# Mixture-of-experts layers of a macaron block: two second-choice scatters under way among the experts, and three experts in place of two that complete the output's rows

## The chip, the cores and the metric

The kernel runs on one core of one Trainium2 chip. A core has a matrix engine (TensorE, here PE, whose weight loads the profile lists as PEld), a vector engine (VectorE, DVE), a scalar engine (ScalarE, ACT), GpSimd (POOL) and SyncE (SP), and 16 DMA engines that they share. Each of the five executes its own queue of instructions in order and waits on semaphores. In this kernel SP issues the plain transfers and POOL the indirect ones (rows scattered or gathered by an index for each partition).

The metric is the device time of one execution, in microseconds (us): the median of several runs. A profiled execution gives the trace; its own time stands beside it.

## The reference

A macaron block: a feed-forward layer with weight 0.5, a gated delta-rule attention, and the same feed-forward layer again. The two feed-forward layers are mixtures of 8 experts; each token goes to its two best experts, and every choice has a capacity of 640 tokens for each expert. The part that the change touches is this, with N = 4096 tokens, D = 128 and a hidden width of 512:

```python
capacity = max(int(N / E * CAPACITY_FACTOR), 1)              # 640
top_k_probs, top_k_idx = jax.lax.top_k(router_probs, TOP_K)  # 2 choices
out = jnp.zeros_like(x_flat)
for k in range(TOP_K):
    eid, ew = top_k_idx[:, k], top_k_probs[:, k]
    ...
    pos = jnp.take_along_axis(pos_all, eid[:, None], axis=1)[:, 0]
    valid = pos < capacity
    disp = jnp.zeros((E, capacity, D)).at[eid, pos_c].add(jnp.where(valid[:, None], x_flat, 0.0))
    gate = jax.nn.silu(jnp.einsum('ecd,efd->ecf', disp, wi_gate))
    up = jnp.einsum('ecd,efd->ecf', disp, wi_up)
    expert_out = jnp.einsum('ecf,edf->ecd', gate * up, wo)
    tok_out = expert_out[eid, pos_c]
    out = out + jnp.where(valid[:, None], ew[:, None] * tok_out, 0.0)
...
x = x + 0.5 * _L0_ffn_ref(_layernorm(x), ...)
x = x + _L0_attn_ref(_layernorm(x), ...)
x = x + 0.5 * _L0_ffn_ref(_layernorm(x), ...)
```

## The kernel before

**Layout.** The tokens lie in SBUF as `x`, four groups `g` of 128 partitions x 8 tokens x 128 numbers. Each feed-forward layer ("layer 1" and "layer 2" below) has four tables in HBM: `disp` for each choice `k` (8 experts x 640 slots, a row of 128 numbers, the token's number and its two weights) and `back` for each choice (one row of results for each token).

**Dispatch.** `Routing.dispatch` (L520) sends one tile of 128 tokens to its slots with an indirect scatter on POOL. The slots of different scatters never overlap. To let them run side by side, the table is given as 32 views that count as disjoint (L373); a scatter writes view `(g * NC + n) % abreast`, and two scatters to one view are kept in order by a wait of the second for the landing of the first. With `abreast` at its full value no scatter waits for another; with 1 each waits for the one before it. The first choices are sent in full before the experts begin. The second choices are sent by `second` (L569), with `abreast` 1: in layer 1 eight tiles before expert 0 and then four with each of experts 0 to 5 (`LATER`, L861), in layer 2 four before expert 0 and then three with each of experts 0 to 3 (L1569 to L1578).

**Experts.** `experts` (L554) runs i = 0 to 15: the 8 experts on first choices, then the 8 on second choices. For each, `fetch` (L574) loads the weights `we` (768 KB, three buffers) and the 640 rows `xd` (three buffers), and `expert` (L601) transposes the rows (`ptx`, then `xdT` by ACT and DVE), computes 4 column blocks for each half of the tokens (`pg`, `pu`, `sg`, `hT`), multiplies back (`py`) in two parts of three and two tiles, weights them on DVE (`ye`, L652), and scatters the five tiles on POOL to `back` (L661). The second choices' scatters stand in POOL's queue among these: one after the first three result scatters, the others after the last two. POOL's indirect transfers are held in program order (`in_order`, L516). Expert 8's rows need all second choices landed.

**Combining.** `combine_first` (L548) loads a group of `back` for first choices and adds half of it to `x` on DVE, one group with each of experts i = 10 to 13; the addition stands behind the weighting of the expert before (`weighted`). The second choices' results of layer 1 are added in the attention stage.

**The end.** In layer 2 the last two experts (i = 14, 15) do not write to `back`. Before expert 14, `x` is stored to `kept` in HBM (L1575), and `fetch` gathers for each slot the row of `kept` of its token (`xb`, L586 to L598; both experts' rows and weights are fetched before expert 14 is computed). Within expert 14, after its last `hT`, `finish` (L1587) loads the four groups of `back` of second choices, which hold experts 8 to 13 by then, adds them to `x` and stores the whole output. The last two experts then write `0.5 * weight * py + xb` (L647) over their tokens' rows in the output (L661, to the views `self.final[1]`), so these scatters wait for the output's stores.

**Order on SP.** Loads made by `load` (L230) keep their program order on SP; the plain `xd` loads (L583) and `y` loads (L537) are placed by the scheduler.

Of the kernel before, what the change touches and what calls it, by code (L numbers as in the profile page):

```python
# [26 lines left out]
NW = 14  # L27
VPAD = 31
OUT_OF_RANGE = 1000000

# [125 lines left out]
def macaron_kernel(ctx: ExitStack, tc: tile.TileContext, x_in, consts, wts, w1b, wexp, out):  # L158
# [209 lines left out]
    class Routing:  # L368
# [178 lines left out]

        def combine_first(self, i, ex):  # L548

            g = i - NE - 2  # L550
            if 0 <= g < NG:
                self.add(g, self.results(g, 0, ex.tile([P, NC * D], F32, tag="y", name=f"y{self.layer}_{g}")))

        def experts(self, between):  # L554

            layer = self.layer
            with tc.tile_pool(name=f"ex{layer}", bufs=2) as ex:
                fetched = {}  # L560
                for i in range(2 * NE):
                    among = between(i, ex)

                    for n in (i, i + 1) if self.final and i == 2 * NE - 2 else (i,):
                        if n not in fetched:
                            fetched[n] = self.fetch(ex, *divmod(n, NE))
                    self.expert(ex, *divmod(i, NE), among, *fetched.pop(i))

        def second(self, tiles):  # L569

            for g, n in tiles:
                self.dispatch(g, 1, [n], 1)

        def fetch(self, ex, k, e):  # L574

            nm = f"{self.layer}_{k}_{e}"
            we = ex.tile([P, 3 * FF], F32, tag="we", bufs=3, name=f"we_{nm}")
            load(we, wexp[e])
            xd = ex.tile([P, JS, RW], F32, tag="xd", bufs=3, name=f"xd_{nm}")
            src = disp[self.layer - 1][k][e * ESLOT : (e + 1) * ESLOT, :]  # L580
            src = src.rearrange("(p j) d -> p j d", j=JS)
            if not (self.final and k == 1 and e >= NE - 2):
                nc.sync.dma_start(out=xd, in_=src)  # L583
                return we, xd, None
            load(xd, src)
            xb = ex.tile([P, JS, D], F32, tag="xb", name=f"xb_{nm}")  # L586
            nc.gpsimd.memset(xb, 0.0)
            for j in range(JS):
                self.in_order(nc.gpsimd.indirect_dma_start(
                    out=xb[:, j, :],  # L590
                    out_offset=None,
                    in_=self.final[0],
                    in_offset=bass.IndirectOffsetOnAxis(
                        ap=xd[:, j, D : D + 1].bitcast(I32), axis=0
                    ),
                    bounds_check=NT - 1,
                    oob_is_err=False,
                ))  # L598
            return we, xd, xb

        def expert(self, ex, k, e, among, we, xd, xb):  # L601
            nm = f"{self.layer}_{k}_{e}"
            wo = we[:, 2 * FF :].rearrange("p (f d) -> p f d", d=D)
            xdT = ex.tile([P, ESLOT], F32, tag="xdT", name=f"xdT_{nm}")
            for q, js in enumerate((range(0, 3), range(3, JS))):
                pt = psB(f"ptx_{nm}_{q}")
                w = len(js) * P
                for i, j in enumerate(js):
                    nc.tensor.transpose(pt[:, i * P : (i + 1) * P], xd[:, j, :D], ident)  # L609
                to = xdT[:, js[0] * P : js[0] * P + w]  # L610
                if q % 2 == 0:
                    nc.scalar.copy(to, pt[:, :w])  # L612
                else:
                    nc.vector.tensor_copy(to, pt[:, :w])
            if xb is not None:
                half = ex.tile([P, JS], F32, tag="half", name=f"half_{nm}")
                nc.vector.tensor_scalar(half, xd[:, :, D + 1 + k], 0.5, None, ALU.mult)
            hT = ex.tile([P, 4, ESLOT], F32, tag="hT", name=f"hT_{nm}")

            def up(f, s0, w):  # L620
                pg = psA(f"pg_{nm}_{s0}_{f}")
                nc.tensor.matmul(  # L622
                    pg[:, :w], lhsT=we[:, f * P : (f + 1) * P], rhs=xdT[:, s0 : s0 + w],
                    start=True, stop=True,
                )
                pu = psA(f"pu_{nm}_{s0}_{f}")
                nc.tensor.matmul(  # L627
                    pu[:, :w], lhsT=we[:, FF + f * P : FF + (f + 1) * P],
                    rhs=xdT[:, s0 : s0 + w], start=True, stop=True,
                )  # L630
                sg = ex.tile([P, w], F32, tag="sg", bufs=3, name=f"sg_{nm}_{s0}_{f}")
                nc.scalar.activation(sg, pg[:, :w], AF.Silu)  # L632
                made = nc.vector.tensor_tensor(hT[:, f, s0 : s0 + w], pu[:, :w], sg, ALU.mult)  # L633
                self.made = getattr(made, "ins", made)

            def down(js, among):
                py = psB(f"py_{nm}_{js[0]}")
                ye = ex.tile([P, len(js), D], F32, tag=f"ye{len(js)}", bufs=3, name=f"ye_{nm}_{js[0]}")
                for i, j in enumerate(js):
                    for f in range(4):  # L640
                        nc.tensor.matmul(  # L641
                            py[:, i * P : (i + 1) * P], lhsT=hT[:, f, j * P : (j + 1) * P],
                            rhs=wo[:, f, :], start=(f == 0), stop=(f == 3),
                        )
                if xb is not None:
                    for i, j in enumerate(js):
                        weighted = nc.vector.scalar_tensor_tensor(  # L647
                            ye[:, i, :], py[:, i * P : (i + 1) * P], half[:, j : j + 1], xb[:, j, :],
                            ALU.mult, ALU.add,
                        )  # L650
                else:
                    weighted = nc.vector.tensor_tensor(  # L652
                        ye, py[:, : len(js) * P].rearrange("p (j d) -> p j d", d=D),
                        xd[:, js[0] : js[0] + len(js), D + 1 + k].unsqueeze(2).to_broadcast(
                            [P, len(js), D]
                        ),
                        ALU.mult,
                    )
                self.weighted = getattr(weighted, "ins", weighted)
                for i, j in enumerate(js):  # L660
                    self.in_order(nc.gpsimd.indirect_dma_start(  # L661
                        out=self.final[1][(e - NE + 2) * JS + j] if xb is not None else self.rows_[k][e * JS + j],
                        out_offset=bass.IndirectOffsetOnAxis(
                            ap=xd[:, j, D : D + 1].bitcast(I32), axis=0
                        ),
                        in_=ye[:, i, :],
                        in_offset=None,
                        bounds_check=NT - 1,
                        oob_is_err=False,
                    ))  # L670
                self.second(among)

            if k == 0 or e < NE - 1:
                for s0 in (0, ESLOT // 2):
                    for f in range(4):
                        up(f, s0, ESLOT // 2)
                if xb is not None:
                    self.final[2](ex)
                down(range(0, 3), among[:1])
                down(range(3, JS), among[1:])  # L680
            else:

                for f in range(4):
                    up(f, 0, 3 * P)
                for f in range(2):
                    up(f, 3 * P, 2 * P)
                down(range(0, 2), ())
                for f in range(2, 4):
                    up(f, 3 * P, 2 * P)
                down(range(2, 3), ())  # L690
                down(range(3, JS), ())
# [172 lines left out]
    def between_1(i, ex):  # L864

        if i == 0:
            r1.second(later[: LATER[0]])

        if i in (NE + 1, NE + 2):
            clear_slots(1, i - NE - 1)  # L870
        if i in (NE + 3, NE + 4):
            clear_back(1, i - NE - 3)
        r1.combine_first(i, ex)
        return later[sum(LATER[: i + 1]) : sum(LATER[: i + 2])]
# [695 lines left out]

    def between_2(i, ex):
        if i == 0:
            r2_.second(rest[:4])
        r2_.combine_first(i, ex)
        if i == 2 * NE - 2:  # L1575
            for g in range(NG):
                load(by_group(kept[:, :])[g], x[:, g].rearrange("p n d -> p (n d)"))
        return rest[4 + 3 * i : 7 + 3 * i]  # L1578
# [13 lines left out]
            r2_.add(g, ys[g], r2_.made)  # L1592
            load(out[g], x[:, g])

    r2_.final = kept[:, :], dram_disjoint_views(out.rearrange("g p n d -> (g p n) d"), 2 * JS), finish
    r2_.experts(between_2)


# [85 lines left out]
```

## Time and profile before

| | us |
|---|---|
| median of 5 runs | 1014.78 |
| lowest, highest | 1001.78, 1020.41 |
| profiled execution | 1008.41 |
| its span | 1006.6 |
| PE busy in the span | 848.0 (84%) |
| DVE busy | 515.1 (51%) |
| ACT busy | 362.9 (36%) |
| POOL busy | 303.0 (30%) |

In the profiled execution layer 1's routing takes the first 70 us, its experts run from 74 to about 320 us, the attention to about 740 us, and layer 2's experts from 756 to 999 us. The costliest groups of POOL are the scatters of rows (L524, 128 of 991 ns) and of results (L661, 150 of 972 ns to `back`, 10 more to the output).

The profile can be read as a page (busy time of each engine, the chain of waits that ended last, groups of instructions), as busy time in chosen stretches, as a list of who waited for whom, and as instructions in order of time. In the last, a line has the start, the length, the engine, the source line, the operation, what it writes and reads, how many were merged, and in brackets the idle time of the engine before it and what ended that. "issue" is time in which the engine waited for nothing that the profile shows. PE's matmuls are pipelined and their ends are modelled. A DMA's line is the time of its issue, not of its transfer.

### The profile page before, as it was taken

The numbers are of one execution on the slowest core, as the hardware profiler recorded it, in microseconds if no ns is written. First come the engines' busy times: TensorE is split into PE (matmuls) and PEld (weight loads), VectorE is DVE, ScalarE is ACT, GpSimd is POOL, SyncE is SP. The second block draws the span as 40 slices with busy tenths as digits, with TensorE's granted clock in tenths as the row PEclk, the third lists the DMA queues.
The fourth block names the chain that finished last, engine by engine and source line by source line (L and its number), as shares of the span: only waits on it lengthen the run. The fifth ranks groups of instructions, "written<-read, shape, count | busy, mean of one in ns | idle before, by whom it ended". The sixth has DMA issues, their size and how long they took to land.

```text
span 1006.6 us, 19407 instructions
## 1 busy us (share of the span) xinstructions
PE 848.0 (84%) x7674; PEld 585.1 (58%) x7674; DVE 515.1 (51%) x1218; ACT 362.9 (36%) x710; POOL 303.0 (30%) x321
## 2 busy tenths in 40 slices
PE   3459989899995899899989989899319999999975
PEld 1247776677774344563565455455206777777754
DVE  5533333234432349579848967966623334344442
ACT  5422222122222534726724662255612223222211
POOL 2664553533225000000023003200343553332363
PEclk9999999989999799999999989999758999999998
DMA  9832425396211140320140002300042333344451
GB/s 311 306 107 75 120 85 149 127 378 217 88 54 42 33 104 1 95 47 1 49 110 26 11 13 60 80 2 2 22 126 79 106 101 114 100 147 157 147 180 46
DMA packets 36778, 101.11 MB, mean 100 GB/s; under 512 B 9296, under 2 KB 11831, under 8 KB 36688
## 3 DMA queue, kind: packets, MB, share of 16 engines
q1 hardware_dynamic: 27152, 82.47, 26.4%
q0 software_dynamic: 9536, 17.41, 5.4%
q8 instruction: 60, 0.98, 0.4%
q14 instruction: 30, 0.25, 0.1%
HBM read 48.31 MB, written 42.39 MB: 90 GB/s over the span
## 4 chain that ended last, share of the span: by engine, by line
PE 50%; issue 16%; DVE 13%; POOL 7%; ACT 6%; DMA 4%; SPq 2%; another core or an unknown queue 1%; POOLq 0%; DVEq 0%; ACTq 0%
PE pg L622 9%; PE pu L627 9%; PE py L641 8%; PE pms L1332 4%; POOL disp L524 3%; POOL back L661 3%; PE pjq L977 2%; DVE inv L1109 1%; DVE add L1104 1%; DMA disp<-row,send 1%; PE pjk L977 1%; SPq L1219 1%; PE pc L1243 1%; PE pyo L1513 1%
## 5 line engine op out<-in xcount | busy, mean ns | idle before, releaser
L524 POOL DMA_INDIRECT disp<-row,send x128 | 126.9, 991 | 477.7 <-ACT tz L1126 177.8
L633 DVE TENSOR_TENSOR hT<-pu,sg 128x320 f32<-128x320 f32 (+2 forms) x256 | 125.5, 492 | 182.1 <-PE pu L627 123.4
L661 POOL DMA_INDIRECT back<-ye,xd x150 | 145.7, 972 | 195.6 <-DVE ye L652 157.2
L622 PE MATMUL pg<-xdT,we 128*128 128x320 f32 (+2 forms) x512 | 188.0, 450 | 15.0 <-ACT xdT L612 13.8
L627 PE MATMUL pu<-xdT,we 128*128 128x320 f32 (+2 forms) x512 | 183.8, 441 | 0.8 <-issue 0.8
L632 ACT ACTIVATE sg<-pg 128x320 f32<-128x320 f32 (+2 forms) x256 | 111.6, 437 | 193.9 <-PE pg L622 117.1
L641 PEld LDWEIGHTS py<-we,hT 128*128 128x128 f32 x1280 | 148.7, 192 | 10.7 <-issue 4.4
L641 PE MATMUL py<-we,hT 128*128 128x128 f32 x1280 | 149.6, 275 | 5.3 <-issue 4.1
L622 PEld LDWEIGHTS pg<-xdT,we 128*128 128x128 f32 x512 | 96.9, 195 | 60.7 <-ACT xdT L612 21.5
L627 PEld LDWEIGHTS pu<-xdT,we 128*128 128x128 f32 x512 | 99.5, 195 | 43.8 <-issue 5.0
L1332 PE MATMUL pms<-vlag,lagw 128*32 128x512 f32 x832 | 108.3, 595 | 0.5 <-issue 0.5
L652 DVE TENSOR_TENSOR ye<-py,xd 128x256 f32<-128x256 f32 (+2 forms) x61 | 29.5, 486 | 101.2 <-PE py L641 82.1
L612 ACT COPY xdT<-ptx 128x384 f32<-128x384 f32 x32 | 15.3, 479 | 174.7 <-PE ptx L609 166.8
L1332 PEld LDWEIGHTS pms<-vlag,lagw 128*32 128x32 f32 x832 | 27.9, 108 | 40.5 <-issue 36.4
L609 PE MATMUL ptx<-cst,xd 128*128 128x128 f32 x160 | 24.5, 287 | 24.4 <-DMA xd<-disp 24.4
L1109 DVE TENSOR_TENSOR inv<-inv,add 128x31 f32<-128x31 f32 (+15 forms) x124 | 42.5, 343 | 3.8
L1104 DVE TENSOR_TENSOR add<-sys,inv 128x31 f32<-128x31 f32 (+15 forms) x124 | 42.2, 340 | 3.8
L1258 DVE TENSOR_TENSOR ui<-pc,cst 128x512 f32<-128x512 f32 x32 | 22.1, 689 | 25.6 <-PE pc L1250 19.8
L609 PEld LDWEIGHTS ptx<-cst,xd 128*128 128x128 f32 x160 | 19.6, 148 | 24.9 <-issue 24.9
L1302 ACT COPY delta<-po 128x128 f32<-128x128 f32 x32 | 8.5, 266 | 69.2 <-PE po L1295 65.7
L977 PE MATMUL pjk<-hT,wc 128*128 128x512 f32 x64 | 29.5, 603 | 0.6 <-DVE bt L361 0.6
L341 PE MATMUL pt_r<-cst,row 128*128 128x128 f32 x64 | 16.5, 388 | 14.7 <-ACT row L330 13.7
(225 smaller groups left out, 1038.2 us busy)
## 6 DMA issues: line engine op xcount, KB each, us to landing
we<-in_wexp_dram SPq DMA_DIRECT2D x32, 768.0 KB
disp<-empty SPq DMA_DIRECT2D x4, 2620.0 KB
xd<-disp SPq DMA_DIRECT2D x32, 327.5 KB
back<-zero SPq DMA_DIRECT2D x4, 2048.0 KB
y<-back SPq DMA_DIRECT2D x16, 512.0 KB
back<-ye,xd POOLq DMA_INDIRECT x150
vlag<-vbl SPq DMA_DIRECT2D x16, 143.5 KB
vlag<-vbl SPq DMA_DIRECT2D x16, 143.4 KB
```

Of the source, the lines that this page charges most:

```text
L524: sent = nc.gpsimd.indirect_dma_start(out=self.slots[k][(g * NC + n) % abreast], out_offset=bass.IndirectOffsetOnAxis(ap=send[:, k, :], ax ...
L609: nc.tensor.transpose(pt[:, i * P : (i + 1) * P], xd[:, j, :D], ident)
L622: nc.tensor.matmul(pg[:, :w], lhsT=we[:, f * P : (f + 1) * P], rhs=xdT[:, s0 : s0 + w], start=True, stop=True,)
L627: nc.tensor.matmul(pu[:, :w], lhsT=we[:, FF + f * P : FF + (f + 1) * P], rhs=xdT[:, s0 : s0 + w], start=True, stop=True,)
L632: nc.scalar.activation(sg, pg[:, :w], AF.Silu)
L633: made = nc.vector.tensor_tensor(hT[:, f, s0 : s0 + w], pu[:, :w], sg, ALU.mult)
L641: nc.tensor.matmul(py[:, i * P : (i + 1) * P], lhsT=hT[:, f, j * P : (j + 1) * P], rhs=wo[:, f, :], start=(f == 0), stop=(f == 3),)
L661: self.in_order(nc.gpsimd.indirect_dma_start(out=self.final[1][(e - NE + 2) * JS + j] if xb is not None else self.rows_[k][e * JS + j], ou ...
L977: nc.tensor.matmul(pj_.tile, lhsT=wc[:, i, k, :], rhs=hT[:, :, l0 : l0 + P], start=(k == 0), stop=(k == KQ - 1),)
L1104: nc.vector.tensor_tensor(add, sys_[:, j, k:].unsqueeze(2).to_broadcast([P, r, k]), iv[:, j, :k].unsqueeze(1).to_broadcast([P, r, k]), ALU ...
L1109: nc.vector.tensor_tensor(iv[:, k:, :k], iv[:, k:, :k], add, ALU.add)
L1332: nc.tensor.matmul(pm_[i].tile[32 * tile_ : 32 * tile_ + 32, :], lhsT=lagw[:, q, u, :], rhs=vl[:, q, :, l0 : l0 + 128], start=first, stop= ...
```

## The change

1. `second` takes `abreast`, 2 if not given: the second choices among the experts alternate between two views of the table, so each waits for the last but one. The tiles sent before expert 0 keep `abreast` 1 in both layers.
2. `combine_first` adds the four groups with experts i = 9 to 12, in both layers.
3. `LASTS = 3`: the last three experts (i = 13, 14, 15) complete the output's rows. `kept` is stored before expert 13, the rows and weights of all three are fetched and the rows of `kept` gathered there (15 gathers for 10, three buffers of `xb`), `finish` runs within expert 13 alone, and the output has 15 views for 10. `back` then holds experts 8 to 12.

```diff
+LASTS = 3
...
         def combine_first(self, i, ex):
-            g = i - NE - 2
+            g = i - NE - 1
...
-                    for n in (i, i + 1) if self.final and i == 2 * NE - 2 else (i,):
+                    for n in range(i, 2 * NE if self.final and i == 2 * NE - LASTS else i + 1):
...
-        def second(self, tiles):
+        def second(self, tiles, abreast=2):
             for g, n in tiles:
-                self.dispatch(g, 1, [n], 1)
+                self.dispatch(g, 1, [n], abreast)
...
-            if not (self.final and k == 1 and e >= NE - 2):
+            if not (self.final and k == 1 and e >= NE - LASTS):
                 nc.sync.dma_start(out=xd, in_=src)
                 return we, xd, None
             load(xd, src)
-            xb = ex.tile([P, JS, D], F32, tag="xb", name=f"xb_{nm}")
+            xb = ex.tile([P, JS, D], F32, tag="xb", bufs=LASTS, name=f"xb_{nm}")
...
-                        out=self.final[1][(e - NE + 2) * JS + j] if xb is not None else self.rows_[k][e * JS + j],
+                        out=self.final[1][(e - NE + LASTS) * JS + j] if xb is not None else self.rows_[k][e * JS + j],
...
-                if xb is not None:
+                if xb is not None and e == NE - LASTS:
                     self.final[2](ex)
...
         if i == 0:
-            r1.second(later[: LATER[0]])
+            r1.second(later[: LATER[0]], 1)
...
         if i == 0:
-            r2_.second(rest[:4])
+            r2_.second(rest[:4], 1)
         r2_.combine_first(i, ex)
-        if i == 2 * NE - 2:
+        if i == 2 * NE - LASTS:
             for g in range(NG):
                 load(by_group(kept[:, :])[g], x[:, g].rearrange("p n d -> p (n d)"))
...
-    r2_.final = kept[:, :], dram_disjoint_views(out.rearrange("g p n d -> (g p n) d"), 2 * JS), finish
+    r2_.final = kept[:, :], dram_disjoint_views(out.rearrange("g p n d -> (g p n) d"), LASTS * JS), finish
```

## The prediction

> **What bounds the kernel now.** I read the chain of waits first, then the busy time by stage, then the order of time on POOL, SP and PE where a stage is longer than its neighbours. Experts are numbered as in the loop, i = 0 to 15; expert i begins with its `ptx` transposes.
>
> The chain by engine, from the page:
>
> ```profile
> PE 50%; issue 16%; DVE 13%; POOL 7%; ACT 6%; DMA 4%; SPq 2%; another core or an unknown queue 1%; POOLq 0%; DVEq 0%; ACTq 0%
> ```
>
> PE carries half of the chain, but POOL and DMA have 11%, so somewhere the scatters end last. Busy time by stage, each stretch cut at the start of an expert's `ptx` (columns: stretch, length, busy time and instructions of PE, PEld, DVE, ACT, POOL, granted clock, DMA share, GB/s):
>
> ```profile
> 90.96:133.75 42.79, 41.74 (x234) 33.42 (x233) 15.68 (x33) 11.93 (x27) 25.09 (x26) 1.00 0.37 109
> 147.99:166.42 18.43, 15.58 (x79) 12.01 (x78) 5.25 (x11) 3.98 (x9) 9.78 (x11) 0.91 0.34 98
> 166.42:181.98 15.56, 13.89 (x79) 11.12 (x78) 5.72 (x12) 3.98 (x9) 4.93 (x6) 1.00 0.84 264
> 181.98:200.71 18.73, 14.06 (x79) 11.12 (x78) 5.68 (x12) 3.98 (x9) 9.74 (x11) 0.97 0.21 60
> 200.71:217.43 16.72, 16.57 (x77) 12.75 (x78) 4.92 (x10) 3.98 (x9) 6.56 (x7) 0.83 1.02 356
> 773.41:944.30 170.89, 166.69 (x927) 133.32 (x925) 66.91 (x135) 47.31 (x108) 69.94 (x73) 1.00 0.38 117
> 958.54:979.50 20.96, 15.25 (x79) 11.31 (x78) 9.31 (x14) 3.98 (x9) 16.44 (x15) 1.00 0.51 175
> 979.50:995.25 15.75, 14.32 (x78) 11.16 (x77) 6.62 (x18) 3.98 (x9) 7.03 (x8) 1.00 0.30 111
> ```
>
> The clean price of an expert is 170.89 / 12 = 14.24 us (experts 1 to 12 of the second routed layer), and PE sets it. Layer 1 pays more four times: expert 5 +4.19, expert 6 +1.32, expert 7 +4.49, expert 8 +2.48 (this one at a granted clock of 0.83), together 12.5. In the last layer expert 14 pays +6.72 and the last expert, which also drains, 15.75 in all.
>
> Why expert 7's stretch is long, in order of time:
>
> ```profile
> 165.52 0.97 POOL L524 DMA_INDIRECT disp<-row,send  x1 [0.30 <-issue]
> 168.78 0.97 POOL L524 DMA_INDIRECT disp<-row,send  x1 [2.29 <-DMA disp<-row,send]
> 176.94 0.97 POOL L524 DMA_INDIRECT disp<-row,send  x1 [7.19 <-DMA disp<-row,send]
> ...
> 194.31 0.97 POOL L524 DMA_INDIRECT disp<-row,send  x1 [3.00 <-DMA disp<-row,send]
> ...
> 197.44 0.32 SPq L583 DMA_DIRECT2D xd<-disp  x1
> ...
> 200.71 1.30 PE L609 MATMUL ptx<-cst,xd 128*128 128x128 f32 x5 [4.20 <-DMA xd<-disp]
> ```
>
> Each second-choice scatter waits for the one before it to land. The last of 32 starts at 194.31, so expert 8's rows are read at 197.44 and PE stands still until 200.71; its clock is then low, which is expert 8's own +2.48. Between 66 and 200 us POOL waits 54.4 us in 20 such waits.
>
> The end, where the output is completed:
>
> ```profile
> 965.52 1.86 SPq L232 DMA_DIRECT2D y<-back  x4
> ...
> 974.89 4.62 DVE L544 SCALAR_TENSOR_TENSOR x<-y,x 128x1024 f32<-128x1024 f32 x4
> ...
> 984.46 1.02 POOL L661 DMA_INDIRECT out_dram<-ye,xd  x1 [5.21 <-DVE hT L633]
> ...
> 995.10 0.97 POOL L661 DMA_INDIRECT out_dram<-ye,xd  x1 [1.93 <-DVE ye L647]
> ```
>
> POOL does wait 5.21 us for the output's rows, but seven scatters later it has caught up and waits 1.93 us for `ye`, that is for PE. So the end is set by PE's delay in expert 14, not by POOL's queue.
>
> **Part 1: two scatters under way among layer 1's experts.** No instruction is added. Per expert POOL issues 5 result scatters and 4 second-choice ones, one each 1.275 us: 9 x 1.275 = 11.5 us, under 14.24. Chained, the third and fourth each wait for a landing: start to start 3.46 and 3.46 us (99.95, 103.41, 106.87), 2.92 and 3.27 (115.81, 118.73, 122.00), at worst 3.26 and 8.16. So a round of POOL takes 15.1 to 20.4 us (first result scatters at 92.06, 108.15, 123.27, 140.77, 157.86, 178.22, 195.58), 103.5 for six against PE's 85.4. That is the 18 us by which the seconds come late. With two views in turn the third waits for the one issued three places earlier (3.8 us), normally landed; the fourth waits for the second, issued 2.55 us earlier, so it waits 2.92 - 2.55 = 0.4 to 3.46 - 2.55 = 0.9 us. The round is 11.9 to 12.4 us and POOL keeps step with PE: expert 5's `ye` comes at 89.37 + 5 x 14.24 = 160.6, its last second-choice scatter ends about 173, expert 8's `xd` can be read near 176 and lands 3.3 later (197.44 to 200.71). PE wants it at 90.96 + 7 x 14.24 = 190.6. Slack 11 us, so expert 8's wait goes.
>
> Bounds: at least 4.49 + 2.48 = 6.97 us is gained, if experts 5 and 6 stall again: in the view of waits PE stands there for `xdT`, ACT and DVE for PE or an unnamed releaser, and the one landing named (a second-choice scatter, 5.3 us before `ye`) writes nothing that `ye` reads. At most 12.5, if they do not recur; so far they cost nothing of their own, since 200.71 was set by the scatters anyway. I take the middle, 9.8. A third bound, nothing, would hold if two scatters in flight land no sooner than two in a row. Against it: result scatters, which no chain holds, start every 1.275 us, and the last first-choice scatter, issued at 749.45 after eight others at that pace, had landed by 751.79, when the read of `xd` is issued.
> [...]
>
> In layer 2 only 12 seconds are left among experts, and experts 1 to 12 already run at 14.24: gain 0, POOL's waits lie beside PE. The `abreast=1` heads of both layers are unchanged.
>
> **Part 2: `combine_first` one expert earlier.** The same four DVE additions (1.23 us each) and loads. In layer 1 the first now stands in DVE's queue behind expert 8's `ye`, about 205.5 by the new time (190.6 + 14.24 + 0.6), with expert 9's `xdT` and `hT` queued behind it. Its load waits for expert 7's result scatters, which now go out from about 190 to 196 and land near 198 (in layer 2 the last starts at 877.45 and the load at 879.67). Before, that load was issued at 214.03 beside a 2 MB clear, and the trace's landing marks put it between 221 and 224, some 10 us; in layer 2, alone, it took 3.4. So it lands between 201 and 208: cost 0 to 2.5. I take 0; the cover is the clear, issued after expert 7 (about 191), having mostly drained by 200. In layer 2 the load landed at 883 and the addition will be due at 887.9: 0.
>
> **Part 3: three experts complete the rows.** Added: one memset of 0.63 us at 733.5, where POOL idles; 5 gathers of 1.30 us; five DVE operations every 0.26 us for two of 0.56 and 0.42; 0. Moved: on SP the four `kept` stores, in order with the weights, now stand ahead of expert 13's weights and rows, and the fourth waits for an addition that ends about 931.9. So `we` of expert 13 goes from 916.01 to about 932.3. The same bundle a period later (fourth `kept` at 946.11, two `we`, one `xd`, 2.4 MB) had landed by 954.9 by the marks, 8.7 us; so 941 against the first `pg` at 945.4. Slack 4 us, cost 0; without cover 3 to 5. Gathers: 15 from 949.9, right behind expert 12's scatters, to 969.4; expert 13's result rows queue behind them on POOL until then, with nobody on PE waiting.
>
> The loads of `y` follow the last result scatter of the expert before, as they did: scatter 963.21, load 965.52; now 948.65 and about 951.5. The additions follow expert 13's last `hT` (954.35) as they followed expert 14's. So the stage with its +6.72 keeps its shape and moves one expert earlier: 0 on the sum. It can vanish (-6.7), if it came from chance, or grow by the 5 more gathers beside it (+6.5). The 5.21 us wait of POOL goes, but it was not late at the end.
>
> **Sum.** -9.8 + 0 + 0 + 0. The profiled execution took 1008.41 (span 1006.6): 998.6. It is 6.4 below the median of the five runs, 1014.78, and nothing says that the change acts otherwise there: 1014.8 - 9.8 = 1005.0. With the bounds of part 1 alone 1002.3 to 1007.8.
>
> **Rivals.** (a) The tail's stall goes too: -13.7 to -19.2, 996 to 1001. For it: of PE's idle in that stall the view of waits puts 4.1 us down to "issue", to no other engine. Against: loads, gathers and additions keep their distances. Chance 0.12. (b) The expected gain does not come, or the tail gives it back: two scatters under way land at the old pace, or +6.5 in the tail eats the 6.97: -3 to +4, 1012 to 1019. For it: landing took 8.16 us beside the weights and a clear; against: quiet steps of 2.9 to 3.5. Chance 0.20. (c) Slower: DVE waits in the first layer's `combine_first`. If `y` still lands at 224, DVE stands from 205.5 on, PE runs on for the two column blocks that its four banks hold (2.1 us) and then waits 16.4: 12.5 are won before and 16.4 lost, +4, or with the tail's +6.5 about +10: 1019 to 1025. It decides when `y` lands after about 220. Against: its releaser, expert 7's scatters, comes 12 us earlier. Chance 0.16. The forecast keeps 0.52.
>
> **Numbers.** Five runs spread over 18.6 us, so about 1% (10 us) is what a measurement can tell from no change. The forecast's 7 to 12.5 lies across that line, a little over half above with (a): faster 0.41. Same 0.46: the rest of the forecast, most of (b), part of (c). Slower 0.13. Range 996 to 1022: it takes in (a), (b) and half of (c).
>
> **What would show it.** Right: POOL's waits for `disp` between 66 and 200 us fall from 54.4 to below 30; expert 8's `ptx` has no wait for `xd` and its stretch is 14.24 at clock 1.00; the stretch of expert 13 or 14 is still about 21, and expert 15's `ye` still ends the last scatter's wait. Wrong: a wait of several us before the first addition at L544 in layer 1 (c); POOL rounds still over 15 us (b); expert 13's `pg` waiting for `we` (part 3); the finishing stage near 14.24 (a).

## The result, and the profile after

| | before | after |
|---|---|---|
| median | 1011.22 us (86 runs) | 1008.4 us (44 runs) |
| profiled execution | 1008.41 us, span 1006.6 | 1010.52 us, span 1008.7 |

Run against run the ratio is 1.0017, 95% [1.0, 1.0035]: no change, where 9.8 us of gain was forecast. The ratio takes only the runs within 1.5% of the fastest of their kernel (53 of 86 before, 42 of 44 after), so it can stand above 1 while the median of all runs is 2.8 us lower after. The two traces, cut at the same places, show that 3.3 us were won in layer 1, a third of the forecast, and that the end gave back more than the whole gain:

| stretch of the span | before | after | difference |
|---|---|---|---|
| start to expert 0 of layer 1 | 74.02 | 72.15 | -1.87 |
| layer 1, start of expert 0 to start of expert 15 | 228.86 | 225.56 | -3.30 |
| to expert 0 of layer 2 | 453.38 | 452.68 | -0.70 |
| layer 2, start of expert 0 to start of expert 13 | 188.04 | 187.56 | -0.48 |
| start of expert 13 to PE's last instruction ("the tail" below) | 50.95 | 59.57 | +8.62 |
| from there to the last instruction | 11.35 | 11.18 | -0.17 |

The chain by engine, from the page of the changed kernel. POOL's share fell from 7% to 2% and PE's rose from 50% to 63%: the scatters hardly stand on the chain any more.

```profile
PE 63%; DVE 10%; issue 9%; ACT 6%; DMA 5%; SPq 2%; POOL 2%; another core or an unknown queue 2%; POOLq 0%; DVEq 0%; ACTq 0%
```

What POOL waits for between 60 and 260 us (us in all, times, the longest): 54.4 us in 20 waits for `disp` before, now

```profile
POOL disp L525 <- DMA disp<-row,send: 27.0, 13, 5.1
```

Busy time by stage, cut at experts' `ptx` as before (stretch, length, busy time and instructions of PE, PEld, DVE, ACT, POOL, granted clock, DMA share, GB/s): expert 2, experts 4 and 5, and experts 6 to 14 of layer 1; ten clean experts of layer 2; then experts 13, 14 and 15:

```profile
103.93:124.86 20.93, 16.78 (x77) 11.37 (x78) 5.90 (x12) 3.87 (x9) 10.47 (x11) 0.92 0.30 89
...
139.61:169.54 29.93, 28.57 (x156) 22.30 (x155) 10.68 (x22) 7.96 (x18) 17.49 (x19) 1.00 0.38 114
169.54:297.71 128.17, 125.02 (x695) 100.08 (x694) 52.24 (x103) 35.73 (x81) 47.61 (x50) 1.00 0.54 183
795.54:937.95 142.41, 138.91 (x772) 111.20 (x771) 57.90 (x116) 39.77 (x90) 53.85 (x57) 1.00 0.41 130
937.95:960.44 22.49, 16.19 (x79) 12.00 (x78) 9.32 (x14) 3.98 (x9) 17.61 (x17) 0.90 0.76 271
960.44:983.12 22.68, 17.95 (x78) 13.18 (x79) 6.59 (x18) 3.98 (x9) 9.07 (x10) 0.72 0.10 29
983.12:997.52 14.40, 14.05 (x79) 11.09 (x77) 5.86 (x14) 3.98 (x9) 6.87 (x8) 1.00 0.09 26
```

The wait at expert 8 is gone: 128.17 / 9 = 14.24 us for each expert from 6 on. In return expert 2 is 6.69 us too long, at first with the clock at 1.00 (to 116, then 0.57 to 120). At the end two experts take 22.5 and 22.7 us where one took 20.96. In order of time, the end of the changed kernel:

```profile
944.15 1.04 POOL L590 DMA_INDIRECT xb<-kept,xd  x1 [0.30 <-issue]
...
952.42 4.62 DVE L545 SCALAR_TENSOR_TENSOR x<-y,x 128x1024 f32<-128x1024 f32 x4
952.56 1.38 PE L642 MATMUL py<-we,hT 128*128 128x128 f32 x10 [1.01 <-issue]
...
956.85 0.37 PE L642 MATMUL py<-we,hT 128*128 128x128 f32 x1 [1.82 <-issue]
...
961.87 0.68 PE L610 MATMUL ptx<-cst,xd 128*128 128x128 f32 x2 [0.35 <-issue]
963.59 0.99 POOL L590 DMA_INDIRECT xb<-kept,xd  x1 [0.30 <-issue]
966.23 1.38 DVE L648 SCALAR_TENSOR_TENSOR ye<-py,half,xb 128x128 f32<-128x128 f32 x5 [9.18 <-remote]
966.37 0.48 ACT L613 COPY xdT<-ptx 128x384 f32<-128x384 f32 x1 [15.39 <-remote]
966.90 1.43 PE L623 MATMUL pg<-xdT,we 128*128 128x320 f32 x2 [4.35 <-ACT xdT L613]
```

POOL gathers without a break from 944.15 to 964.58. From 952.5 on PE's matmuls of `py` come late, some of them one at a time, with idle time that is put to "issue", so to nothing that the profile shows. The additions stand back to back (4.62 us for four), so DVE isn't waiting for `y` here. PE is not alone in standing: by the profile PE's `ptx` is done at 962.55, but ACT copies it to `xdT` only at 966.37, and DVE begins `ye` at 966.23, both about 1.7 us behind the last gather's end and for a releaser that the profile doesn't name ("remote"). PE then waits 4.35 us for `xdT`. `ye` reads gathered rows, `xdT` reads none, so a late landing of the rows would explain the first and not the second. Behind that the clock is low: expert 14 runs at 0.72.

### The profile page after: what moved, and what is told of

Its sections match the earlier page's. It is cut to its first block, busy times and chain, and to the rows that moved or that the text cites. A ratio compares the mean times of both kernels' runs of the same rounds, so it can differ in the third digit from the quotient of the medians.

```text
span 1008.7 us, 19424 instructions
## 1 busy us (share of the span) xinstructions
PE 852.9 (85%) x7674; PEld 588.3 (58%) x7674; DVE 516.0 (51%) x1222; ACT 362.8 (36%) x710; POOL 309.1 (31%) x327
## 4 chain that ended last, share of the span: by engine, by line
PE 63%; DVE 10%; issue 9%; ACT 6%; DMA 5%; SPq 2%; POOL 2%; another core or an unknown queue 2%; POOLq 0%; DVEq 0%; ACTq 0%
PE pg L623 14%; PE pu L628 13%; PE py L642 12%; PE pms L1333 5%; PE pjq L978 2%; DMA w1f<-in_w1b_dram 2%; PE pjk L978 2%; SPq L233 2%; DVE inv L1110 1%; DVE add L1105 1%; ACT xdT L613 1%; PE ptx L610 1%; POOL back L662 1%; PE pc L1244 1%
## 5 line engine op out<-in xcount | busy, mean ns | idle before, releaser
L662 POOL DMA_INDIRECT back<-ye,xd x145 | 140.9, 972 | 214.3 <-DVE ye L653 178.4
L978 PE MATMUL pjq<-hT,wc 128*128 128x512 f32 x64 | 28.7, 598 | 0.1
```

The source lines that it names most:

```text
L662: self.in_order(nc.gpsimd.indirect_dma_start(out=self.final[1][(e - NE + LASTS) * JS + j] if xb is not None else self.rows_[k][e * JS + j] ...
L978: nc.tensor.matmul(pj_.tile, lhsT=wc[:, i, k, :], rhs=hT[:, :, l0 : l0 + P], start=(k == 0), stop=(k == KQ - 1),)
```

## The experiments

Five batches ran, each on one chip with its own runs of the kernel before. The chips differ. In batches 1, 2, 3 and 5 the kernel before takes 986 to 993 us; in batch 4 it takes 1008.7, about as in the first measurement (1011.2). "Clean" means 14.24 us an expert.

Theory T going in: two abreast is worth about what was forecast, and the end gives it back. Two readings of the end: **G**, the burst of 15 gathers holds PE up; **Y**, DVE stands in the additions for `y`, and `ye`, `xdT` and `hT` queue behind them. A third reading: what the first profile shows belongs to its chip. Each chip was used in one batch, so chip and time can't be told apart; "chip" below means both. What a run is off the kernel before, in microseconds, is worked out from its ratio; differences between two runs are those of their medians.

### Batch 1: the parts (kernel before 992.89 us)

**e1**, the kernel before, and only this:

```diff
-        def second(self, tiles):
+        def second(self, tiles, abreast=2):
...
-                self.dispatch(g, 1, [n], 1)
+                self.dispatch(g, 1, [n], abreast)
...
-            r1.second(later[: LATER[0]])
+            r1.second(later[: LATER[0]], 1)
```

(and the same 1 for layer 2's head).

> The kernel before with part 1 alone (second choices two abreast among the experts). Theory T (part 1 gains in layer 1, part 3 loses it again at the end): layer 1 from expert 1's ptx to expert 10's takes 3 to 12 us less than the 140.7 of before, the tail from expert 13's ptx to PE's end stays near 51 us, and the median is 0.4% to 1% below before (ratio 0.990 to 0.996). Rival R (part 1 gains nothing in the median, because stalls of PE that no scatter causes take the place of the wait): ratio 0.998 to 1.002.

977.34 us, 0.9878 [0.9833, 0.9924], 12.1 us off, more than theory T had. Layer 1 is clean from expert 1 on, and so is the tail (44.24 us for the 51 expected), with 10 gathers in it.

**e2**, the whole change with two completing experts:

```diff
-LASTS = 3
+LASTS = 2
```

> The changed kernel with LASTS = 2: parts 1 and 2 without part 3. Theory T: as the first run, ratio 0.990 to 0.996, tail near 51 us with the long stretch at expert 14. Rival R: 0.998 to 1.002. If part 2 costs something by itself, this one is above the first run by more than 0.2%, with a wait before an addition at the combining line.

980.07 us, 0.9892 [0.9857, 0.9926]. Combining one expert earlier costs nothing that these runs resolve. Here too the long stretch at expert 14 is missing: the tail is 45.8 us, with 2.0 us lost in expert 13.

**e3**, the whole change with one scatter under way:

```diff
-        def second(self, tiles, abreast=2):
+        def second(self, tiles, abreast=1):
```

> The changed kernel with every second choice's scatter behind the last (abreast 1): parts 2 and 3 without part 1. Theory T: the tail from expert 13's ptx to PE's end is 57 to 62 us (59.6 with the change, 51.0 before), the ratio 1.005 to 1.010, that is slower than both. Rival R: 0.999 to 1.003, like the change.

996.31 us, 1.0056 [1.0024, 1.0088]: without part 1 the rest makes the kernel slower. The ratio is the one expected, but not for the reason given: the tail is 47.2 us and not 57 to 62, and the profiled execution loses 19.0 us in layer 1's experts 7 to 9. In order of time, layer 1 of this run:

```profile
195.63 1.30 PE L610 MATMUL ptx<-cst,xd 128*128 128x128 f32 x5 [11.91 <-DMA xd<-disp]
...
216.86 1.22 DVE L545 SCALAR_TENSOR_TENSOR x<-y,x 128x1024 f32<-128x1024 f32 x1 [3.51 <-DMA y<-back]
...
218.87 1.17 PE L628 MATMUL pu<-xdT,we 128*128 128x320 f32 x2 [2.12 <-DVE hT L634]
```

Expert 8 waits 11.91 us for its rows. The first addition, now one expert earlier, waits 3.51 us for `y`, and PE 2.12 us behind it: rival (c)'s mechanism. It is there when the scatters are late. With two abreast the first addition waits for `y` in two profiles only, 0.3 us in e4 and 0.8 in e18, and PE loses nothing by it.

**e4**, the whole change without the gathers:

```diff
-            for j in range(JS):
+            for j in ():
```

> The changed kernel with the 15 gathers of kept's rows left out (xb stays zero, so the last three experts' rows lack their x). Theory G (the burst of gathers holds PE up, directly): the stretches of experts 13 and 14, 22.5 and 22.7 us with the change, fall to 14.2 to 16 each, the tail to 43 to 47 us. Rival Y (the loads of y, the four additions and the output's stores hold DVE and through it PE): the stretches stay at 19 or more for one of the two, the tail at 50 or more.

976.27 us, 0.986 [0.9809, 0.991], tail 42.9 us. This speaks for G, but e1's tail is clean with 10 gathers, so on this chip 10 do little; the whole change was not run beside it.

### Batch 2: the tail (kernel before 986.17 us)

**e5**, the whole change as it is:

> The whole change once more, beside its parts on one chip. Theory S (the three completing experts cost what two abreast gain): ratio 0.995 to 1.003 to the kernel before, and 8 to 12 us above the run with two abreast alone, with a tail (start of expert 13 to PE's end) of 57 to 60 us. Rival C (the tail's 59.57 us in the first profile belong to PE's slow phases on that chip, and the three experts cost little by themselves): 0.988 to 0.991 here, as the version with two experts had (0.9892), with a tail of 43 to 48 us.

978.30 us, 0.9931 [0.9891, 0.9972]: the same kernel that gained nothing in the first measurement gains here. Its tail is 47.2 us, so rival C of the expectation holds, though the ratio lies a little above the one it gave. The chain of its end, and then DVE and PE in order of time:

```profile
924.15 8.84 DMA y<-back
943.72 4.46 PE py L642 x40
```

```profile
927.16 1.23 DVE L545 SCALAR_TENSOR_TENSOR x<-y,x 128x1024 f32<-128x1024 f32 x1 [1.40 <-DMA y<-back]
929.67 1.22 DVE L545 SCALAR_TENSOR_TENSOR x<-y,x 128x1024 f32<-128x1024 f32 x1 [1.29 <-DMA y<-back]
...
934.22 1.38 DVE L648 SCALAR_TENSOR_TENSOR ye<-py,half,xb 128x128 f32<-128x128 f32 x5
...
936.38 0.81 PE L623 MATMUL pg<-xdT,we 128*128 128x320 f32 x2 [2.36 <-DVE hT L634]
```

Here Y is seen: the additions wait for landings, PE waits 2.36 us for `hT`, and behind that, from 937.63 to 940.83, its pairs of matmuls start every 1.07 us, where from 941.41 on it is every 0.54 (granted clock 0.91 over the whole stretch). Together 18.56 us for expert 14, +4.3. `ye` follows the additions without a wait, while POOL still gathers until 941.67: what stood still in the first profile doesn't here.

**e6**, e1 once more:

> The kernel before with two scatters abreast and nothing else, again. Both theories: 0.983 to 0.992, since layer 1's experts stay at 14.24 us. If the slow phases of PE come here too (an expert of over 18 us at its granted clock of 1.00 before the slow phase), they are not due to the three experts; if they come in the run of the whole change alone, they are.

977.53 us, 0.991 [0.9874, 0.9946], tail 43.9 us, so only 0.8 us below e5. The reason is POOL, in the chain's last line:

```profile
947.57 3.90 DMA xb<-kept,xd
```

With two experts the gathers and scatters of POOL end last, 13.3 us behind PE's end; with three it is 11.2 us. So here part 3 costs 3.3 us in PE's tail and gives 2.1 back behind it.

**e7**, the whole change without the loads and additions of `y`:

```diff
-        ys = [ex.tile([P, NC * D], F32, tag="yz", bufs=NG, name=f"y2_{g}_1") for g in range(NG)]
-        for g in range(NG):
-            load(ys[g], by_group(back_[1][1][:, :])[g])
         for g in range(NG):
-            r2_.add(g, ys[g], r2_.made)
             load(out[g], x[:, g])
```

> The whole change, with the loads of the second choices' results and their additions to x left out of the finishing step (the output's rows are stored without them, so that part of the sum is missing). Theory Y (DVE stands in the additions, waiting for landings, and the next expert's xdT and hT queue behind it): the tail falls to 43 to 46 us with all 15 gathers in place. Theory G (the 15 gathers in one burst delay PE): the tail keeps the excess it has in the run of the whole change, within 3 us.

972.51 us, 0.9864 [0.9785, 0.9944], tail 42.9 us with all 15 gathers in place. So on this chip the gathers alone don't hold PE up: Y.

**e8**, e4 once more:

> The whole change without the 15 gathers, so that the last three experts' rows lack x, beside the whole change on one chip. Theory G: the tail is 43 us and the whole is faster than the whole change by the excess that its tail shows (4 to 16 us). Theory Y: the additions still wait for landings, the tail keeps at least 3 us over 43, and the difference to the whole change is under 3 us.

972.12 us, 0.9864 [0.9785, 0.9944]. In the profile expert 14 is 18.25 us long without any gather (PE waits 2.06 us for `hT`), so Y comes without gathers too. But the profiled execution is the slowest of the five: 979.41 us, where the others take 971.8 to 972.9. The median is 6.2 us below e5, more than Y allowed and about as much as e7 saves, and e4, the same kernel, has a clean tail. So whether the gathers make `y` land late on this kind of chip stays open.

### Batch 3: where the additions stand (kernel before 988.27 us)

**e9**, the whole change:

> The whole change, beside three of its variants on one chip. Theory Y: expert 14 begins late by 2 to 5 us (its pg waits for hT, behind additions that wait for y), the tail (start of expert 13 to PE's end) is 46 to 48 us, and the chain of waits at the end names a load of y; ratio 0.988 to 0.996. If this chip shows PE's slow phases as the first profile did, the tail is 57 to 60 us, no wait is named for most of it, and the ratio is 0.997 to 1.004.

978.11 us, 0.9898 [0.9859, 0.9937], tail 47.7 us, with the load of `y` (9.48 us) on the chain.

**e10**, e1:

> The kernel before with two scatters abreast alone, for comparison. Theory Y with POOL at the end: PE's tail is 43 to 45 us, the last instruction comes 13 us after PE's end (11 us in the whole change), since ten gathers and ten scatters in POOL's queue end last; ratio 0.986 to 0.993. On a chip with slow phases of PE: below the whole change by 5 us or more if three experts cost it, within 3 us if they do not.

976.78 us, 0.9892 [0.9859, 0.9926], tail 44.0 us, end 13.2 us behind PE's.

**e11**, the whole change with the additions spread. The stores of groups 2 and 3 then follow expert 13's output scatters, so that its part in those rows is written over.

```diff
                     for f in range(4):
                         up(f, s0, ESLOT // 2)
+                        if xb is not None and e == NE - LASTS + 1 and s0 == 0 and f % 2:
+                            self.final[2](ex, (2 + f // 2,))
...
-                    self.final[2](ex)
+                    self.final[2](ex, (0, 1))
...
+    def finish(ex, groups):
...
-        for g in range(NG):
+        for g in groups:
             r2_.add(g, ys[g], r2_.made)
             load(out[g], x[:, g])
```

> The whole change with the finishing step's four additions spread: two where they stand, behind expert 13's last hT, one each behind the second and the fourth hT of expert 14. Theory Y: PE no longer stands for hT at expert 14, the tail falls from 47 to 43 to 44.5 us, the last instruction stays 11 us behind PE's end, and the kernel is 2 to 4 us below the whole change and 1 to 3 us below two abreast alone: ratio 0.984 to 0.991. Rival (the tail's excess is the three experts' gathers, stores and loads together, not where the additions stand): within 1 us of the whole change.

978.32 us, 0.9899 [0.9862, 0.9937]. The tail is clean (42.9 us), as Y has it, but the time is that of e9. Two stores had to wait for expert 13's scatters, and POOL waited for them (the profile names `ye`, but this `ye` was made by 946.4; SP's last store goes out at 952.07):

```profile
955.99 0.97 POOL L662 DMA_INDIRECT out_dram<-ye,xd  x1 [6.08 <-DVE ye L648]
```

The end came 16.7 us behind PE's: what PE won, POOL lost.

**e12**, the kernel before with part 3 alone (`LASTS = 3`, one scatter under way, `g = i - NE - 2` in `combine_first`):

> The kernel before with three completing experts alone: scatters one at a time, combine_first where it was. Theory: layer 1 keeps its excess of about 12 us, with no wait of DVE for y at expert 9 (which the version that also combined earlier had); the tail costs 2 to 4 us over the kernel before's own on this chip and POOL's end gives 2 back: ratio 0.998 to 1.005. Rival (three experts cost most of what two abreast gain): 1.006 to 1.012.

991.01 us, 1.0031 [0.9992, 1.0071]. Layer 1 has only 1.9 us of excess in this execution, against 19.0 in e3's, so chained scatters cost very different amounts (e12's runs lie between 983 and 999 us, e9's between 976 and 980). And part 3 leans on part 2, as SP and PE in order of time show:

```profile
924.93 0.38 SPq L233 DMA_DIRECT2D we<-in_wexp_dram  x1
...
931.50 1.30 PE L610 MATMUL ptx<-cst,xd 128*128 128x128 f32 x5 [8.62 <-DMA xd<-disp]
```

The last addition of first choices ends at 924.50, `kept` is stored only then, expert 13's weights and rows stand behind it on SP, and PE waits 8.62 us.

### Batch 4: a chip like the first (kernel before 1008.74 us)

**e13**, the whole change:

> The whole change, once more, as the base of this batch. Without slow phases of PE: 0.988 to 0.995, tail 46 to 48 us with the load of y on the chain. With them (first layer's experts over 15 us at a granted clock of 1.00, tail of 57 to 60 us): 0.997 to 1.004, as in the first measurement.

1007.98 us, 1.0017 [0.998, 1.0055], tail 57.9 us, as in the first measurement.

**e14**, without the gathers, as e4:

> The whole change without the 15 gathers (the last three experts' rows lack x). If slow phases come in the run of the whole change: theory G (PE's instructions come late beside a long burst of POOL's indirect transfers) has this tail at 43 to 47 us with no idle time of PE without a named wait; rival (those phases come from something else) keeps such a phase in the tail. Without slow phases: 42 to 47 us in both, which tells nothing new.

991.83 us, 0.9842 [0.9771, 0.9914], 16.2 us below e13's median.

**e15**, e11 with expert 13's output scatters held back until the last store is issued, so that the output is complete again:

```diff
-                for i, j in enumerate(js):
+                def send(i, j):
                     self.in_order(nc.gpsimd.indirect_dma_start(
...
+                for i, j in enumerate(js):
+                    if xb is not None and e == NE - LASTS:
+                        self.held.append((send, i, j))
+                    else:
+                        send(i, j)
...
                             self.final[2](ex, (2 + f // 2,))
+                            for send, i, j in self.held if f == 3 else ():
+                                send(i, j)
```

> As e11, and expert 13's output scatters stand behind the last output store in the program, so that the stores no longer wait for them. Theory Y with POOL at the end: PE's tail stays at 43 us (14.24 us at expert 13 and 14), POOL idles under 3 us behind expert 13's scatters, the last instruction is 10 to 12 us behind PE's end, and the time is 2 to 5 us below the whole change and 1 to 4 below two abreast alone: 0.983 to 0.989. Rival (POOL's 15 gathers and 15 scatters end last anyway): within 1 us of the whole change, with the last instruction over 13 us behind PE's end.

1009.05 us, 1.002 [0.9983, 1.0057], tail 61.8 us: both numbers missed. On this chip the place of the additions is not what matters; whether it wins on the others was not tried.

**e16**, e1:

> Two abreast alone, as the base for the version with spread additions. Without slow phases: 0.986 to 0.992, PE's tail 43 to 45 us and the last instruction 13 us behind PE's end. With slow phases: theory G says they come in the first layer (its scatters run without pause there) and, with ten gathers for fifteen, less long in the tail than in the whole change: below it by 3 to 8 us.

998.88 us, 0.994 [0.99, 0.9979]: faster than both kernels, 9.1 us below e13 (3 to 8 were expected).

The tails of the three, by stage (columns as above; experts 13, 14, 15): first e14 with no gather, then e16 with 10, then e13 with 15:

```profile
939.90:954.14 14.24, 13.89 (x79) 11.12 (x78) 7.24 (x12) 3.98 (x9) 4.45 (x5) 1.00 0.68 235
954.14:968.82 14.68, 14.17 (x80) 11.03 (x79) 7.81 (x18) 3.98 (x9) 4.87 (x5) 1.00 0.45 174
968.82:983.22 14.40, 14.05 (x79) 11.09 (x77) 6.59 (x17) 3.98 (x9) 7.78 (x8) 1.00 0.09 27
```

```profile
937.90:952.14 14.24, 13.89 (x80) 11.12 (x78) 6.76 (x14) 3.98 (x9) 4.46 (x6) 1.00 0.61 216
952.14:973.07 20.93, 15.94 (x80) 11.82 (x78) 9.32 (x14) 3.98 (x9) 15.75 (x15) 0.94 0.58 209
973.07:989.22 16.15, 16.01 (x77) 12.19 (x77) 6.61 (x17) 3.98 (x9) 7.86 (x8) 0.87 0.19 65
```

```profile
935.22:956.53 21.31, 16.55 (x79) 12.78 (x78) 9.32 (x14) 3.97 (x9) 16.74 (x16) 0.92 0.75 265
956.53:978.66 22.13, 15.94 (x79) 12.28 (x78) 6.59 (x18) 3.97 (x9) 9.84 (x11) 0.77 0.15 49
978.66:993.07 14.41, 14.05 (x79) 11.09 (x77) 5.86 (x14) 3.98 (x9) 6.87 (x8) 1.00 0.09 26
```

43.3, 51.3 and 57.9 us: on this chip 10 gathers cost PE 8.0 us over the tail without any and 15 cost 14.5, so 0.8 to 1.0 us each, in the expert beside which they run and the one behind it. (The 10 are those of e16, another kernel; on the other chips its tail is 43.9 to 44.2 us, and against that they cost about 7.) Without them the loss is gone, with the loads, additions and stores all in place. Here it is G. The profile of e13 repeats the first one: the last gather ends at 961.75, DVE begins `ye` at 963.41 and ACT `xdT` at 963.55, and PE waits 5.36 us for it.

### Batch 5: pace or company (kernel before 992.30 us)

**e17**, the whole change with a pause between gathers:

```diff
             for j in range(JS):
+                if j or e > NE - LASTS:
+                    pause = ex.tile([P, 2 * JS * D], F32, tag="pause", bufs=1, name=f"pause_{nm}_{j}")
+                    self.in_order(nc.gpsimd.memset(pause, 0.0))
```

> The whole change, with a fill of a scratch tile (128 x 1280) on POOL between any two of the 15 gathers, so that they start about 2.6 us apart and not 1.30. If PE is held up by gathers that follow one another without pause, the tail (start of expert 13 to PE's end) on a chip that shows the slow phases falls from 58 to 60 us to under 52, with no idle time of PE of over 1 us put to nothing; if each gather costs PE about 1 us whatever the pace, it stays at 56 us or more. POOL's end comes up to 18 us later in both, so the ratio is 1.00 to 1.02 there. On a chip without slow phases the tail is 46 to 62 us by late ye alone, and this run tells nothing about pace.

987.96 us, 0.9959 [0.9935, 0.9983], tail 49.6 us, with the end 18.3 us behind PE's. The tail's loss has named waits, as the expectation has it for a quiet chip: PE stands 2.38 and 0.90 us for `hT`, behind additions that wait for `y` and a `ye` that waits 0.62 us for a gather.

**e18**, e7 once more:

> The whole change without the second results' loads and additions in the finishing step (that part of the sum is missing). On a chip with slow phases: if the burst of gathers alone holds PE up, the tail stays at 55 us or more and the ratio at 0.994 to 1.003; if it needs the loads and stores beside it, the tail is under 48 us and the ratio under 0.990. On a chip without: tail 43 us, ratio 0.983 to 0.990, as in e7.

974.51 us, 0.983 [0.9785, 0.9874], tail 42.9 us. This chip shows no slow phases of PE, so both runs leave the question open for which they were sent: whether gathers at a slower pace, or without traffic beside them, would spare PE.

## Why the prediction was wrong

**The step that failed** is part 3's: "the stage with its +6.72 keeps its shape and moves one expert earlier: 0 on the sum". The +6.72 was not a shape that moves along. On a chip of the first measurement's kind it is the price of the gathers that run beside it, and part 3 raises them from 10 to 15. The term is +8.62 in the first pair of profiles and 57.85 - 51.32 = 6.5 in PE's tail of batch 4, where whole change and two abreast alone stand 9.1 us apart. The text held the right number as its upper bound ("grow by the 5 more gathers beside it (+6.5)"), and took 0. It had the trace to choose by: PE's loss in expert 14 and the 10 gathers lie in the same 15 us, and POOL's end was argued instead. In the first pair of profiles the second failed term is part 1's -9.8, which measured -3.30.

**Part 1, two abreast.** The mechanism was right: POOL's waits fell to 27.0 us (under 30 was forecast), expert 8 waits for nothing, and DVE does not wait for `y` in layer 1's `combine_first`. The size held on the quieter chips: 0.9878, 0.991 and 0.9892 of the kernel before, 8.9 to 12.1 us for the forecast 7.0 to 12.5. That may be luck in part: no profile of the kernel before was taken there, and with one scatter under way layer 1's excess was 19.0 us in e3 and 1.9 in e12, where the sum had 12.5. In batch 4 it was 0.994, 6.1 us with an interval of 2.1 to 10.1, and in the first profile layer 1 gave 3.3. There POOL's indirect transfers, now with fewer pauses, stand beside a PE that pays 6.69 us in expert 2 and 0.5 to 0.95 in each of experts 3 to 5. That term was missing from the sum; that the transfers cause it there is argued from the tail and was not tried in layer 1.

**Part 2, combining earlier.** 0 with two abreast, as forecast; its rival (c) was real but lives only where the scatters are late (e3). That part 3 needs it was not said: without it expert 13 waits 8.62 us (e12). With it, expert 13's weights were issued at 925.93 for the 932.3 reckoned, in a layer that began 5.87 us sooner, and PE did not wait for them.

**Y**, which the prediction had only for layer 1, is what part 3 costs PE in the profiles of the quiet chips: 3.3 to 3.7 us in the tail (e5, e9), of which about 2 come back because POOL ends sooner. That gain the prediction denied ("it was not late at the end"): with PE held up it wasn't, with a clean PE it is.

So rival (b) came true in its second form, the tail that gives the gain back; it had a chance of 0.20. On two quiet chips the whole change gained 6.8 us (e5) and 10.1 (e9), near the 9.8 of the forecast, which was made from a trace of the other kind.

## What to carry to other kernels

When one stage is longer than its neighbours, ask first what else runs in just that stretch and scale the loss with it; a stall that grows with a transfer's count, as here from 8.0 us beside 10 gathers to 14.5 beside 15 (e16 and e13 against e14), moves and grows with it. Of this change the first part is worth keeping alone: it beat both kernels on the chip where the whole change gives nothing (0.994) and was no slower than the whole change on two others (e6, e10). Before several edits are judged together, measure them apart and on more than one chip: here it hung on the chip whether the whole gained 1% or nothing.

## What the runs showed of the hardware that was not expected

- The changed kernel takes 978 us in two batches (e5, e9) and 1008 in another (e13) and in the first measurement, and the difference isn't a factor on everything: clean experts take 14.24 us on all of them, and the granted clock is 0.953 in e5 and in e13. Of the 30.7 us between the spans of e13 and e5, 22.5 lie in three stretches where POOL issues many indirect transfers: the tail (57.9 against 47.2 us), layer 1's experts (15.2 us for each of experts 3 to 5, with scatters beside them, against 14.24; 4.8 in all) and the first routing (expert 0 starts at 73.0 against 66.0).
- Why PE's instructions come late there is open. The recording differs too: the first two traces and those of batch 4 hold 5272 to 5554 landing marks of DMAs each, the others 8426 to 8709, and 2798 to 2814 marks of other semaphore updates for 3177 to 3193. So a wait that the first put to "issue" or "remote" may have a releaser whose mark is missing.
- Landing: a gather of 128 rows took a median of 5.4 us from issue in e5, a result scatter 2.9 and an output scatter 2.2. With pauses between the gathers (e17, 2.4 us from start to start for 1.3) a gather took 3.6.
- With a wait of 2.4 us for `hT` in it, expert 14 of e5 is 4.3 us over clean: behind the wait PE's pairs of matmuls start every 1.07 us for 3.2 us, where later it is every 0.54.
